# Adding fetched expert rows in the DMA instead of on VectorE, in a one-core macaron layer

## The chip, the core and the metric

The kernel runs on one core of a Trainium2 chip. The core has TensorE (PE, with PEld for its weight loads), VectorE (DVE), ScalarE (ACT), GpSimd (POOL) and SyncE (SP), each with an instruction queue of its own that is worked off in order, and 16 DMA engines that all queues share. SP issues nearly all plain transfers here; POOL issues the indirect ones, whose row addresses come from a tile of indices. The metric is the device time of one execution in microseconds.

## The reference

The input is x with 2 sequences of 4096 tokens and 256 features, in float32. Three blocks are added to it in turn: half of a mixture of experts, a linear attention, and half of the same mixture of experts again.

```python
x = x + 0.5 * _L0_ffn_ref(_layernorm(x), gate_w, w1, w2, w3)
x = x + _L0_attn_ref(_layernorm(x), Wq, Wk, Wv, Wb, ...)
x = x + 0.5 * _L0_ffn_ref(_layernorm(x), gate_w, w1, w2, w3)

def _L0_ffn_ref(x, gate_w, w1, w2, w3):      # 8 experts, two per token
    scores = softmax(xf @ gate_w)
    top_scores, top_idx = top_k(scores, 2)
    scale = zeros((T, E)).at[arange(T)[:, None], top_idx].set(top_scores)
    xs = scale.T[:, :, None] * xf[None, :, :]
    h = silu(einsum('etd,edh->eth', xs, w1)) * einsum('etd,edh->eth', xs, w3)
    y = einsum('eth,ehd->etd', h, w2)
    return y.sum(axis=0)
```

The attention is a gated delta rule with a short convolution and a SiLU in front. It is worked in chunks and carries a state `S` from one chunk to the next.

## The kernel before

The tokens are cut into 16 units. A unit is 256 tokens of each sequence, held as four tiles of 128 tokens with 256 features. For the mixtures of experts, units are put together in groups: 1, 3, 4, 4 and 4 units before the attention (names beginning with `a`), and 4, 4, 4, 3 and 1 after it (names beginning with `b`). A group of one unit is dense: all eight experts run over all its tokens (`all_experts`, L978). Every other group goes through memory in three steps.

- `prepare` (L1041) normalises and routes the tokens. For each of the four tiles of a unit and each of the two choices it makes a tile `row` (the tokens times their score, three buffers under the tag `row`), and an indirect DMA from POOL scatters these rows into `slots` in HBM, so that the rows of one expert lie together (`scatter`, L930).
- `experts` (L1122) loads `slots` two tiles at a time on SP (`xi`), multiplies them with w1 and w3, then with w2, and SP stores the results in `made` in HBM (L1181).
- `combine` (L1183) loads the tokens' own rows `xt` again (L1188). For each tile and each choice, POOL fetches the results of 128 tokens from `made` into a tile `got` with an indirect DMA (`gather`, L948), and DVE adds half of it to the tokens' rows (L1193). `got` shares the tag `row` and its three buffers with the scatter's rows. When all eight fetches of a unit are added, SP stores the block (`leave`, L1032), to `mid1` for the attention or to the output.

There are 30 such units, so 240 scatters, 240 fetches and 240 adds, and every one of them moves 128 rows of 1 KB.

The weights w1, w3 and w2 of all experts lie in one tile `wx_sb`, with w2 in the last 256 columns of each expert. `load_experts` (L676) fills it at the start with five DMAs on SP, and the first dense group is the first to use it. In the dense groups the products with w2 of all experts are summed in PSUM, and one DVE instruction per two tiles adds half of them to the tokens' rows (L1028).

The attention runs beside all this. In it POOL computes powers (`rr` L1498, `nk` L1283, and `rs` L751 for the normalisations) and copies the convolution's carried columns (L1236, L1238). `rr` is the factor that `on` (L1512) applies on DVE before PE transposes `on` into `pto`.

The order of the work is not the order of the source. The instructions are recorded in a `Plan` (L169), step by step, and `Plan.order` (L432) lays them out with costs for each engine (a POOL fetch holds POOL for 1278 ns and lands after 2000 ns plus its size), taking first what has the lowest number among what is ready. The table `TURNS` (L47) adds an offset to that number for each of 1055 steps. An instruction recorded with `either` goes to DVE or ACT, whichever the plan finds free. L202 of the profile is the line of the plan that calls the engines' instructions, and L217, L218, L222 and L223 are the copies placed by `either`; the names of the tiles tell them apart.

Of the kernel before, what the change touches and what calls it, by code (L numbers as in the profile page):

```python
# [36 lines left out]
F32 = mybir.dt.float32  # L37
# [3 lines left out]
ALU = mybir.AluOpType  # L41
# [6 lines left out]
    0: -503, 1: -513, 2: -516, 3: -370, 4: -583, 5: 726, 6: -2518, 7: -130, 8: -302, 9: 87,  # L48
    10: -124, 11: -210, 12: -120, 13: -49, 14: -31, 16: 37, 17: 151, 18: 3947, 19: 159, 20: 180,
    21: 1716, 22: 88, 23: -235, 24: -40, 25: 1464, 26: 884, 27: 1522, 28: 483, 29: 1766, 30: 2462,  # L50
    31: 2582, 32: 3382, 33: 170, 34: -217, 35: 428, 36: -1592, 37: 115, 38: 51, 39: 255, 40: 643,
    41: -669, 42: -210, 43: -509, 44: 505, 45: -127, 46: 91, 47: 1585, 48: 38, 49: 1295, 50: 193,
    51: 1197, 52: 216, 53: -416, 54: 1088, 55: -982, 56: -953, 57: -958, 58: -1515, 59: -1356,
    60: -824, 61: -627, 62: -312, 63: -308, 64: -221, 65: -302, 66: -280, 67: -44, 69: -15,
    70: -62, 71: -145, 72: -50, 73: -46, 74: -1795, 75: -55, 76: -9, 77: 1, 78: 364, 79: 100,
    80: -128, 81: 123, 82: 108, 83: 111, 84: -136, 85: -35, 86: 81, 87: 3, 88: 209, 89: 883,
    90: -104, 91: -82, 92: -14, 93: -22, 94: 222, 95: 298, 96: 1362, 97: 420, 98: -2033, 99: 760,
    100: -48, 101: 25, 102: -85, 103: -2631, 104: -2008, 105: -27, 106: -111, 107: -2148,
    108: 1154, 109: -39, 110: -3637, 111: -2138, 112: -1132, 113: -2221, 114: 21, 115: -1517,
    116: -206, 117: -1803, 118: -1354, 119: -431, 120: -706, 121: 262, 122: -274, 123: -46,  # L60
    124: -191, 125: -192, 126: 422, 127: 1624, 128: 282, 129: 476, 130: -367, 131: 348,
    132: -1154, 133: -780, 134: 44, 135: -614, 136: -460, 137: -333, 138: 67, 139: -480,
    140: -469, 141: -1054, 142: -358, 143: -626, 144: 622, 145: -369, 146: -360, 147: -255,
    148: 396, 149: -432, 150: -147, 151: -170, 152: -32, 153: -7, 154: -43, 156: -10, 157: 68,
    158: -8, 159: 1247, 160: -95, 161: 458, 162: 358, 163: 499, 164: 32, 165: 340, 166: 422,
    167: 647, 168: 198, 169: 492, 170: 549, 171: 500, 173: 576, 174: 1453, 175: 1527, 176: 645,
    177: 427, 178: 1549, 179: 614, 180: -309, 181: 498, 182: -114, 183: -338, 184: 382, 185: -513,
    186: 469, 187: 762, 188: 814, 189: 8, 190: 1130, 191: -495, 192: 370, 193: 2169, 194: -90,
    195: 628, 196: 1176, 197: -53, 198: 2671, 199: 441, 200: 1964, 201: 324, 202: -291, 203: 1998,
    204: 558, 205: -1778, 206: -99, 207: -236, 208: 13, 209: -299, 210: -496, 211: 134, 212: 253,  # L70
    213: -866, 214: 605, 215: -5, 216: -868, 217: 655, 218: -51, 220: 41, 221: 76, 222: -446,
    223: 1126, 224: -1864, 225: -1411, 226: -946, 227: -931, 228: 176, 229: -398, 230: -363,
    231: -1958, 232: -1114, 233: 264, 234: -56, 235: -530, 236: 557, 237: -519, 238: -347,
    239: -51, 240: 158, 241: -137, 242: -215, 243: -234, 244: -269, 245: -136, 246: -433, 247: 23,
    248: -1053, 249: -135, 250: -2056, 251: 123, 252: -1260, 253: -786, 254: -11, 255: -1518,
    256: -135, 257: -1044, 259: -43, 260: 4, 261: 111, 262: 355, 263: -1258, 264: -125, 265: 419,
    266: 246, 267: 83, 268: 66, 269: 30, 270: 282, 271: 48, 272: 342, 273: -585, 274: -1611,
    275: -107, 276: -166, 277: -162, 279: -729, 280: -592, 281: -1401, 282: -604, 283: -383,
    284: -1104, 285: -937, 286: -503, 288: 113, 289: 1177, 290: 546, 291: -209, 292: 350,
    294: 883, 295: 933, 296: 1314, 297: -759, 298: 441, 299: 444, 300: 868, 301: 950, 302: 114,  # L80
    303: 1217, 304: 436, 305: 88, 306: -126, 307: 541, 308: 1618, 309: 165, 310: 2866, 311: 1087,
    312: 359, 313: -25, 314: 931, 315: 29, 316: 922, 317: 115, 318: 1467, 319: 334, 320: 269,
    321: 268, 322: 465, 323: -734, 324: 2, 325: -18, 326: 224, 327: 346, 328: 12, 329: 207,
    330: 396, 331: 306, 332: 432, 333: 157, 334: 385, 335: 124, 336: 384, 337: -18, 338: 1433,
    339: -68, 340: 128, 341: 81, 342: -1578, 343: -120, 344: -552, 345: -466, 346: 1633,
    347: -789, 348: -158, 349: -29, 350: 1347, 351: 264, 352: -603, 353: -1800, 354: 537,
    355: -2390, 356: -2508, 357: -1362, 359: 490, 360: -743, 361: -161, 362: -290, 363: 42,
    364: 1041, 365: -192, 366: 680, 367: -10, 368: -318, 369: -43, 370: 62, 371: 1217, 372: -1254,
    373: -679, 374: -216, 376: -318, 377: -582, 378: 259, 379: -266, 380: -829, 381: -198,
    382: 204, 383: 1523, 384: -80, 385: -1594, 386: 102, 387: -328, 388: -1562, 389: -510,  # L90
    390: 295, 391: -179, 392: -69, 393: 64, 394: -199, 395: -86, 396: -659, 397: -860, 398: -15,
    399: -2434, 400: -685, 401: -25, 402: 145, 403: 49, 404: 284, 405: 540, 406: -1189,
    407: -2502, 408: -477, 409: -171, 410: -99, 411: 80, 412: -220, 413: 272, 414: -816,
    415: -2133, 416: 718, 417: 412, 418: -70, 419: -50, 420: 285, 421: -514, 422: -476, 423: -481,
    424: -17, 425: 1643, 426: 816, 427: -142, 428: 53, 429: -472, 430: -832, 431: 254, 432: -30,
    433: 1608, 434: -459, 435: -605, 436: -98, 437: -309, 438: 368, 439: -500, 440: 105, 441: -73,
    442: -52, 443: 989, 444: 616, 445: 1460, 446: -1346, 447: -1190, 448: -1070, 450: -115,
    451: -291, 452: -772, 453: -91, 454: -1312, 455: -89, 456: -661, 457: 77, 458: 96, 459: 1097,
    460: 788, 461: 234, 462: -284, 463: -255, 464: -109, 465: -503, 466: -526, 467: 881, 468: -35,
    469: 664, 470: 1931, 471: 525, 472: 2711, 473: -124, 475: 169, 476: 2357, 477: 81, 478: 177,  # L100
    479: -167, 480: -547, 481: -142, 482: -101, 483: 1712, 486: -434, 487: 306, 488: 184,
    489: 290, 490: -11, 491: 52, 492: 286, 493: 446, 494: 91, 495: 550, 496: 215, 497: 646,
    498: 1181, 499: 46, 500: -905, 501: -654, 502: 430, 503: -697, 504: -880, 505: -1416,
    506: -120, 507: 500, 508: 298, 509: -2134, 510: 442, 512: -80, 513: -1521, 514: -986,
    515: -723, 516: 79, 517: 243, 518: -198, 519: 76, 520: 124, 521: 84, 522: -178, 523: 367,
    524: 2502, 526: 165, 527: -60, 528: 221, 529: 927, 530: 276, 531: -70, 532: -296, 533: -13,
    534: -67, 535: -712, 536: 128, 537: -170, 538: 120, 539: -9, 540: -30, 541: -107, 542: -148,
    543: -498, 544: 358, 545: -499, 546: -79, 547: 501, 548: 319, 549: -92, 551: 309, 552: -899,
    553: 592, 554: -2484, 555: 11, 556: -499, 557: -256, 558: -129, 559: -452, 560: -116,
    561: -937, 562: 595, 563: 366, 564: -687, 565: 67, 566: 99, 567: -240, 568: 1155, 569: 102,  # L110
    570: -493, 571: -160, 572: 309, 573: 454, 574: -3028, 575: -15, 576: 71, 577: -168, 578: 435,
    580: 550, 581: -178, 582: 1094, 583: -346, 584: -774, 585: 256, 586: 247, 587: -50, 588: -217,
    589: 643, 590: -59, 591: 261, 592: -721, 594: -65, 595: 289, 596: -503, 597: 23, 598: 177,
    599: -106, 600: -96, 601: -347, 602: 123, 603: -91, 604: 533, 605: 204, 606: 230, 607: -692,
    608: -340, 609: -81, 610: -714, 611: 401, 612: 379, 613: 178, 614: -297, 615: 58, 616: 130,
    617: -442, 618: -543, 619: 69, 620: -414, 621: -29, 622: -85, 623: -652, 624: -210, 625: -151,
    626: 189, 627: 31, 628: -71, 629: 102, 630: 122, 631: -395, 632: -4, 633: 162, 634: 204,
    635: 117, 636: -3, 637: 654, 640: -1477, 641: -135, 642: -237, 643: -96, 644: -264, 645: 164,
    646: -221, 647: -180, 649: -591, 650: -24, 651: 771, 652: 121, 653: -16, 654: -717, 655: -79,
    656: 5, 657: 676, 658: 151, 659: -575, 660: -2162, 661: 64, 663: 41, 664: 1075, 665: 464,  # L120
# [431 lines left out]
def kernel(  # L552
# [18 lines left out]
    nc = tc.nc  # L571
    P = 128
    B, L, DM = x.shape
# [1119 lines left out]
```

## Time and profile before

| | |
|---|---|
| time, three runs | median 1911.07 us (1904.27 to 1919.39) |
| the profiled execution | 1918.22 us, its span 1916.4 us |
| mean granted clock of TensorE | 0.934 |
| moved by DMA | 259.48 MB, mean 135 GB/s |
| the queue of POOL's DMAs | 62.95 MB of it |
| POOL, 240 fetches | 241.9 us busy |
| DVE, 240 adds of fetched rows | 101 us busy |

The spans and waits in the text below come from the profiled execution. A row of the trace on POOL is the time in which POOL was busy with a DMA, not the time in which the data moved; when the data has landed is seen from what waits for it. "PE idle" is the length of a stretch minus PE's busy time in it. A wait is put down to the last releaser.

### The profile page before, as it was taken

The page shows a single profiled execution, that of the slowest core. Times are in us where ns is not written, and L with a number is a line of the kernel's source. Part 1 is how long each engine was busy: PE and PEld are TensorE (multiplying, and loading weights), DVE is VectorE, ACT ScalarE, POOL GpSimd, SP SyncE. Part 2 cuts the span into 40 slices and gives each one's busy share as a digit, 9 for nine tenths or more (in the row PEclk, how much of TensorE's full clock was granted, in tenths as well). Part 3 has the DMA queues.
Part 4 walks back from the last instruction along what each step waited for, and adds up shares of the span by engine and source line. Part 5 has one row for each costly group of instructions (what it writes and reads, how often), then busy time and mean ns, then how long its engine had stood idle before and what let it go on. Part 6 is the DMA issues. An engine that isn't in the chain of part 4 may idle for free.

```text
span 1916.4 us, 34449 instructions
## 1 busy us (share of the span) xinstructions
PE 1674.2 (87%) x11656; PEld 1269.5 (66%) x11656; DVE 1238.8 (65%) x4166; ACT 754.5 (39%) x1566; POOL 706.1 (37%) x800
## 2 busy tenths in 40 slices
PE   4878789689989989898999899689899988899898
PEld 2656465566767667676677677567577767777776
DVE  3637568776774795679657667776865777265254
ACT  1435335343343535344443335243352533234332
POOL 2413644453112324623323452331215333353434
PEclk9999989898898989998889989899898999899999
DMA  6173474554132244634223552332246435474673
GB/s 231 50 274 114 167 218 132 176 162 126 49 87 85 79 137 142 188 104 132 78 59 111 158 154 78 114 115 58 67 126 178 130 114 161 156 218 142 203 226 116
DMA packets 296396, 259.48 MB, mean 135 GB/s; under 512 B 117536, under 2 KB 275232, under 8 KB 296224
## 3 DMA queue, kind: packets, MB, share of 16 engines
q1 hardware_dynamic: 271552, 190.13, 32.4%
q0 software_dynamic: 23040, 62.95, 10.1%
q10 hardware_dynamic: 1632, 4.21, 0.6%
q8 instruction: 96, 1.57, 0.3%
q14 instruction: 76, 0.62, 0.1%
HBM read 137.52 MB, written 119.67 MB: 134 GB/s over the span
## 4 chain that ended last, share of the span: by engine, by line
PE 51%; DVE 19%; DMA 11%; issue 9%; ACT 5%; POOL 3%; SPq 1%; another core or an unknown queue 1%; POOLq 0%; ACTq 0%; DVEq 0%
PE po L202 5%; PE pj_a L202 4%; PE pb_a L202 3%; PE p_a L1109 3%; DMA got_b<-made,sli_b 3%; DVE cv_a L202 3%; PE p_b L1109 3%; DMA got_a<-made,sli_a 3%; PE pmid L202 3%; PE py_b L1109 3%; PE py_a L1109 2%; PE pyo L202 2%; PE pg L202 2%; PE pz L202 2%; PE p_b L202 1%
## 5 line engine op out<-in xcount | busy, mean ns | idle before, releaser
L202 DVE SCALAR_TENSOR_TENSOR cv_a<-pre_a,cw_sb,cv_a 128x512 f32<-128x512 f32 x288 | 212.6, 745 | 7.5 <-ACT cv_a L223 3.5
L202 PE MATMUL pj_a<-xT_a,wp_sb 128*128 128x512 f32 x384 | 196.0, 614 | 7.7 <-DVE xT_a L217 2.9
L934 POOL DMA_INDIRECT slots<-row_b,sli_b x120 | 121.2, 1010 | 203.2 <-DVE sli_b L202 78.7
L1109 PE MATMUL p_a<-wx_sb,xiT_a 128*128 x608 | 159.2, 399 | 17.7 <-ACT xiT_a L218 5.2
L934 POOL DMA_INDIRECT slots<-row_a,sli_a x120 | 121.1, 1009 | 126.5 <-issue 49.5
L1109 PE MATMUL p_b<-wx_sb,xiT_b 128*128 x608 | 158.1, 394 | 8.2 <-ACT xiT_b L218 3.8
L952 POOL DMA_INDIRECT got_b<-made,sli_b x120 | 117.7, 981 | 125.8 <-issue 21.8
L952 POOL DMA_INDIRECT got_a<-made,sli_a x120 | 124.2, 1035 | 85.3 <-issue 21.5
L1109 PEld LDWEIGHTS p_a<-wx_sb,xiT_a 128*128 128x128 f32 x608 | 115.4, 199 | 48.4 <-issue 10.9
L1109 PEld LDWEIGHTS p_b<-wx_sb,xiT_b 128*128 128x128 f32 x608 | 110.9, 194 | 31.8 <-ACT xiT_b L218 7.2
L202 POOL TENSOR_TENSOR rr<-ms,mhalf 128x8 f32<-128x8 f32 x32 | 54.2, 1693 | 120.3 <-DVE ms L202 120.1
L1109 PE MATMUL py_a<-wx_sb,hT_a 128*128 x304 | 87.2, 407 | 9.6 <-DVE hT_a L217 2.8
L202 PE MATMUL po<-mid,at 128*128 128x64 f32 x512 | 92.7, 316 | 2.7 <-ACT mid L218 1.4
L202 PEld LDWEIGHTS po<-mid,at 128*128 128x128 f32 x512 | 89.3, 244 | 7.7 <-ACT mid L218 3.8
L202 PE MATMUL pmid<-r,XT 128*128 128x64 f32 x512 | 74.1, 306 | 21.1 <-DVE r L202 9.4
L202 PEld LDWEIGHTS pj_a<-xT_a,wp_sb 128*128 128x128 f32 x384 | 65.0, 193 | 41.1 <-issue 24.4
L202 POOL TENSOR_TENSOR rs_a<-ve_a,mhalf 128x4 f32<-128x4 f32 x32 | 34.2, 1070 | 154.0 <-DVE ve_a L202 153.8
L1109 PE MATMUL py_b<-wx_sb,hT_b 128*128 x304 | 88.0, 412 | 2.2 <-DVE ms L202 0.9
L202 PEld LDWEIGHTS pmid<-r,XT 128*128 128x128 f32 x512 | 70.7, 219 | 28.4 <-DVE r L202 13.0
L202 POOL COPY pre_a<-carry 128x6 f32<-128x6 f32 x96 | 28.7, 299 | 161.5 <-DVE cv_a L202 137.8
L202 DVE TENSOR_TENSOR yb<-yb,z 128x31 f32<-128x31 f32 (+15 forms) x248 | 84.2, 339 | 5.1 <-DVE run_a L202 0.6
L202 DVE TENSOR_TENSOR z<-lb,yb 128x31 f32<-128x31 f32 (+15 forms) x248 | 83.7, 337 | 4.2
(290 smaller groups left out, 3894.2 us busy)
## 6 DMA issues: line engine op xcount, KB each, us to landing
xi_a<-slots SPq DMA_DIRECT2D x76, 256.0 KB
made<-yo_a SPq DMA_DIRECT2D x76, 256.0 KB
xi_b<-slots SPq DMA_DIRECT2D x76, 256.0 KB
made<-yo_b SPq DMA_DIRECT2D x76, 256.0 KB
x_a<-in_L_attn_x_dram SPq DMA_DIRECT2D x32, 256.0 KB
x_a<-mid SPq DMA_DIRECT2D x16, 512.0 KB
xr<-mid SPq DMA_DIRECT2D x64, 128.0 KB
mid<-xr SPq DMA_DIRECT2D x64, 128.0 KB
```

What stands on the lines that cost most here:

```text
L202: self.plan.add(self.name, lambda: real(*args, **kw), ins, outs, cost)
L934: ins = tc.nc.gpsimd.indirect_dma_start(out=dst, out_offset=bass.IndirectOffsetOnAxis(ap=slot, axis=0), in_=row, in_offset=None,)
L952: return tc.nc.gpsimd.indirect_dma_start(out=got, out_offset=None, in_=src, in_offset=bass.IndirectOffsetOnAxis(ap=slot, axis=0),)
L1109: return tc.nc.tensor.matmul(o, lhsT=lhsT, rhs=wx_sb.rearrange("p e c -> p (e c)")[:, cols], start=start, stop=stop,)
```

## The change

The fetch becomes an accumulating DMA: it reads the results from `made` and adds them to the tokens' rows in SBUF. Its destination is the tile of `xt` itself, so `got` and the 240 DVE adds are gone, and the tag `row` is left to the scatters. The factor one half moves into w2: after the load, one instruction multiplies w2 by 0.5 in place, on DVE or ACT, and the dense groups add their sum without a factor. In `combine` the loops over choices and tiles change places, so that the four tiles' first choices are fetched first and then the four second ones. The plan records the fetch with `xt` as a thing read and written. The table TURNS is replaced as a whole by another of the same kind.

```diff
 TURNS = {
-    0: -503, 1: -513, 2: -516, 3: -370, 4: -583, 5: 726, 6: -2518, 7: -130, 8: -302, 9: 87,
...
+    1054: 865,
 }
...
         nc.sync.dma_start(wx_sb[:, :, 2 * KC * FH :], w2.rearrange("e f d -> f e d"))
 
+        down = wx_sb[:, :, 2 * KC * FH :]
+        nc.either.copy(down, down, 0.5)
+
...
-    def gather(g, got, slot):
+    def gather(g, xt, slot):
+
         src = made[g.par][0 : g.ntl * P, :]
 
         def call():
             return tc.nc.gpsimd.indirect_dma_start(
-                out=got,
+                out=xt,
                 out_offset=None,
                 in_=src,
                 in_offset=bass.IndirectOffsetOnAxis(ap=slot, axis=0),
-            )
-
-        plan.add("gpsimd", call, [src, slot], [got], plan.dma(got, 4 * DM, True))
+                compute_op=ALU.add,
+            )
+
+        plan.add("gpsimd", call, [src, slot, xt], [xt], plan.dma(xt, 4 * DM, True))
...
             xa = xt[:, a : a + 2, :]
-            nc.vector.scalar_tensor_tensor(xa, py, 0.5, xa, ALU.mult, ALU.add)
+            nc.vector.tensor_tensor(xa, py, xa, ALU.add)
             yield 1.0
...
             xt = load(g.src, u, f"{g.name}_{i}c")
-            for a in range(NT):
-                for k in range(2):
-                    got = wk.tile([P, DM], F32, tag="row", name=f"got_{g.name}_{i}_{a}_{k}", bufs=3)
-                    gather(g, got, g.slot[i][:, a, k : k + 1])
-                    nc.vector.scalar_tensor_tensor(
-                        xt[:, a, :], got, 0.5, xt[:, a, :], ALU.mult, ALU.add
-                    )
+            for k in range(2):
+                for a in range(NT):
+                    gather(g, xt[:, a, :], g.slot[i][:, a, k : k + 1])
             leave(g, u, xt)
             yield 0.5
```

## The prediction

> **What bounds the kernel now.** I read the busy table first, then the chain of waits, then the stretches in which results are fetched, and last the fetches and what stands around them. Busy time and chain:
>
> ```profile
> PE 1674.2 (87%) x11656; PEld 1269.5 (66%) x11656; DVE 1238.8 (65%) x4166; ACT 754.5 (39%) x1566; POOL 706.1 (37%) x800
> PE 51%; DVE 19%; DMA 11%; issue 9%; ACT 5%; POOL 3%; SPq 1%; another core or an unknown queue 1%; POOLq 0%; ACTq 0%; DVEq 0%
> ```
>
> PE is busy for 87% of the span, so nothing off PE is worth more than the 242 us in which PE stands still, some of them in the start, where weights arrive. The chain's second line names fetched rows twice, at 3% each, some 110 us. They are not worth that: the chain follows the last releaser even where PE is full beside it. So I went to the eight stretches that hold the 240 fetches (found from the POOL rows by time). Columns: length, busy time of PE, PEld, DVE, ACT, POOL with counts, granted clock, DMA share, GB/s.
>
> ```profile
> 227.00:276.00 49.00, 36.76 (x159) 28.59 (x160) 25.74 (x79) 14.16 (x29) 30.64 (x31) 0.85 0.69 212
> 373.00:443.00 70.00, 60.73 (x494) 43.56 (x495) 50.70 (x118) 25.01 (x48) 42.24 (x48) 0.92 0.59 171
> 753.00:816.00 63.00, 55.52 (x384) 39.29 (x383) 38.31 (x91) 23.18 (x47) 42.40 (x44) 0.97 0.62 185
> 1069.00:1145.00 76.00, 70.80 (x639) 55.13 (x637) 44.77 (x114) 24.62 (x51) 43.37 (x46) 0.87 0.56 158
> 1438.00:1520.00 82.00, 75.26 (x534) 56.54 (x532) 53.51 (x133) 28.91 (x58) 41.61 (x48) 0.90 0.55 161
> 1654.00:1716.00 62.00, 56.15 (x417) 46.44 (x415) 35.59 (x116) 21.24 (x46) 35.34 (x35) 0.94 0.69 214
> 1795.00:1856.00 61.00, 54.65 (x275) 43.61 (x274) 27.19 (x90) 24.64 (x52) 32.03 (x33) 0.97 0.80 244
> 1871.00:1909.00 38.00, 34.28 (x160) 26.39 (x161) 18.29 (x52) 10.28 (x31) 23.90 (x24) 1.00 0.41 125
> sum 501.00, PE 444.13 PEld 339.55 DVE 294.09 ACT 172.04 POOL 291.53; mean PE 55.52 PEld 42.44 DVE 36.76 ACT 21.50 POOL 36.44
> ```
>
> In these 501 us PE is idle for 57, or 11%. In the 1333 us between 60 and 1795 us outside them it is busy for 1182, again 11% idle. Fetching starves PE no more than the rest does. Then single rows: the POOL instruction (min/median/max in ns), the queue that carries scatters and fetches, two steps of the chain (start, length), two waits (total, times, longest), the last combine's first and last fetch, and the last add.
>
> ```profile
> L952 POOL DMA_INDIRECT got_b<-made,sli_b x120: 943/958/1282, 1438.6 to 1905.3; - x120
> q0 software_dynamic: 23040, 62.95, 10.1%
> 1810.02 2.46 DMA got_b<-made,sli_b
> 1847.35 6.13 DMA got_b<-made,sli_b
> DVE x_b_0c L202 <- DMA got_b<-made,sli_b: 27.2, 16, 5.6
> PE pto L202 <- DVE on L202: 16.2, 10, 6.8
> 1871.29 0.96 POOL L952 DMA_INDIRECT got_b<-made,sli_b  x1 [16.10 <-DVE hs_b L202]
> 1905.32 0.96 POOL L952 DMA_INDIRECT got_b<-made,sli_b  x1 [0.30 <-issue]
> 1912.33 0.69 DVE x_b15c L202
> ```
>
> A fetch lands 2.5 to 6.1 us after its issue (eight such steps between 1795 and 1853 us, mean 4.6). Back to back, POOL issues one each 0.96 + 0.30 = 1.26 us. The end is close: last fetch at 1905, PE's last product to 1912, span 1916.
>
> **The change part by part.**
>
> Removed, DVE work: 240 adds at 0.42 us (rows of 0.417 to 0.425) are 101 us, a third of DVE's 294 us in the stretches. Removed with them: DVE's in-order waits for fetched rows, 97 us over the eight groups of adds (27.2 above is the largest). They freed no PE: in 1795 to 1856 us DVE waits 27 us for rows, while PE idles 6.4, and of that only 3.1 by DVE (for hs). So I let 40% of the 57 us go, not all: the rest is ACT copies, loads and dependences inside the blocks, which stay. 0.4 x 57 = 23 us. In the first stretch the clock is 0.85 with PE at 75%, against a mean of 0.934; half of the way back on 37 us of PE work is 2 us. Gain 25.
>
> Removed, POOL waits: with three row buffers shared by scatters and fetches, a fetch waits for an add three fetches earlier. The waits of fetches on adds sum to 74 us and on earlier fetches to 15. They go. What is late next is the second choice's fetch: it adds into a row block that the first choice's fetch must have finished. The loop now runs four first choices, then four second ones, so 4 x 1.26 = 5.0 us lie between the two. At a landing of 4.6 nothing waits, at 6.1 it waits 1.1. Behind it on POOL stand the powers for rs, rr and nk and the carry copies, and behind rr waits PE by way of `on` (16.2 us now).
>
> Here the skill speaks against the change. "DMA: Bandwidth & Descriptors", Rules for kernel authors, says that an accumulating DMA reads its destination and writes it later with nothing held in between, so an earlier accumulate's semaphore must be waited for. By the landing row that costs 0 to 1.1 us per unit, 30 units; I take 0.5, so 15 us of POOL, which has 210 us of slack in the stretches: 2 us on the path.
>
> Added, the accumulation itself: no row shows one. Nearest row: the plain fetch, 0.96 us of POOL, and for the transfer 10.1% x 1916 / 480 = 0.40 us of all 16 engines. "Collectives: The Full Stack", in the section on the bandwidth ceiling, says that a DMA's addition costs no cycles but a second source read, with two read descriptors per piece, and that this halves the rate. By the row the change adds nothing. By the rule a transfer takes 0.8 us, 97 us more over 240 in a DMA system at 45% mean share, and the landing is 0.4 later. If POOL writes those descriptors, three in place of two, its 0.96 becomes 1.45 (an estimate from that page and the row). I take the rule for the transfer, the row for POOL. Both ends on POOL stay for the range: 0.96, and double. The engine's addition below the row's cost is excluded, as it moves at least the same bytes.
>
> Stores: SP's store of a finished block used to wait for the last add (76 us in all) and now waits for the last landing. The add and its signal, some 0.5 us, go, 0.4 comes: nothing. Behind it on SP stand the loads of expert rows; PE waits 10.3 us for those today. If landing grew to 9 us, 30 x (9 - 4.6) = 132 us of SP would block; at the 11% by which PE is uncovered, 15 us.
>
> Moved: the first fetch now needs the tokens' rows, which only the first add needed. Their loads go out at 179 us for the fetch at 228, and 1833.8 for 1871.3: hidden by more than 30 us.
>
> Added, the halving of w2: 128 x 2048 in one instruction. By the 128 x 512 scaling of `wo_sb` at 0.48 us, 1.9 on DVE; by four ACT copies of 0.585, 2.3. The first product with w2 is at 49.8 us, and DVE idles 18.7 us before 31.6. Hidden; standing behind w2's arrival on the wrong engine it costs up to 2.3. I take 1. The dense adds keep their shape and time: nothing.
>
> The order: TURNS is another table, so every engine's queue is another order of the same work. No row prices that. Bound: a fifth of the 151 us of PE idle outside the stretches either way, 30 us; value 0.
>
> Sum: -25 + 2 + 1 = -22 on the profiled execution's 1918.22 us, or 1896. That execution lies 7 us above the median of 1911.07, so the median should come to **1889 us**.
>
> **The rivals.**
>
> The fetch becomes dear on POOL (slower). Place: the last combine. From 1871.3 to 1916.4 there are 45 us; the last landing (4.6) and store (3.4, from the last add's end at 1913.0) take 8 of them, so 24 fetches have 37 us, 1.55 us each. Above that step POOL sets the end. At 2.2 us a step (0.96 doubled, with the 0.30) the tail runs 24 x 2.2 - 37 = 16 over. The three densest stretches of 32 fetches (61 to 63 us) overrun by some 8 each, 25; later rr, rs and nk powers cost PE about as much again as it waits behind `on` today, 16. With the gain spent: 1911 + 57 = 1968. For it: three descriptors, unknown software. Against it: POOL is at 58% in the stretches, and the plain fetch leaves 0.29 us to spare.
>
> PE keeps its time: the DVE and POOL waits were under PE's cover, and an awkward order or late landing (15 us above) takes the rest. 1911 - 22 + 17 = 1906. For it: 11% idle inside and outside alike.
>
> The change doesn't do what it says: accumulations into quarters of one block are kept apart as if they hit the same bytes, eight landings in a row, 8 x 5 = 40 us a unit; the tail alone grows from 37 to 120. About 2000 or more. Little speaks for it: the two halves of such a block are already loaded by separate DMAs.
>
> **How the numbers follow.** Likeliest, fetch near today's price: 0.45, own range 1858 (60% of the idle time gone, 11 us more, and 20 us of the order's 30) to 1905, of which 0.05 falls within 1%. PE keeps its time: 0.18, within 1%. Dear fetch: 0.33, 1930 to 2000. Serial fetches: 0.04. A measurement here can tell about 1%, 19 us, from no change. Faster 0.40, same 0.23, slower 0.37. The range runs from that **1858** to **1972**, which takes in the dear fetch at 1968; outside are a very good order (0.07) and the worse dear and serial cases (0.13).
>
> **What would show it.** Right: no `got` tiles, DVE busy near 1138 us, POOL rows of the fetch at 0.96 to 1.45 us, landings under 6.5, PE idle in the stretches near 34 us, waits on earlier fetches under 20 us in all. Wrong: POOL rows of the fetch near 2 us, the last fetch later than 1912 us with PE done, second fetches waiting 3 us and more each, or DVE and POOL relieved as said and PE's idle time unchanged.

## The result and the profile after

The changed kernel takes 2087.86 us (median of 4 runs, 2080.43 to 2089.88), beside 1907.67 us for the kernel before on the same chip (4 runs): a ratio of 1.097, 95% interval 1.089 to 1.105. That is 180 us slower, where 22 us faster was forecast. The profiled execution of after took 2086.84 us, with a span of 2084.9 us.

Busy time, the queue that carries scatters and fetches, and the chain by engine, from the page of after:

```profile
PE 1694.6 (81%) x11656; PEld 1284.4 (62%) x11656; DVE 1151.4 (55%) x3925; ACT 751.6 (36%) x1568; POOL 832.4 (40%) x800
q0 software_dynamic: 46080, 62.95, 14.5%
PE 43%; DVE 18%; issue 13%; POOL 12%; DMA 8%; ACT 4%; SPq 1%; another core or an unknown queue 0%; POOLq 0%; DVEq 0%; ACTq 0%
```

DVE lost 87 us of work; the adds that went had been 101 us, so some of its other rows grew. POOL gained 126 us with the same 800 instructions, the queue moved the same 62.95 MB in twice as many packets, and POOL's share of the chain went from 3% to 12%. PE does the same 11656 products and stands still for 390 us, against 242.

The row of one of the fetch groups, in min/median/max ns, and three waits behind POOL's small powers (total, times, longest, in us):

```profile
L959 POOL DMA_INDIRECT x_b_1c<-made,sli_b x32: 1531/1541/1549, 1540.5 to 2063.8; - x32
```

```profile
DVE x_b L205 <- POOL rs_b L205: 59.3, 5, 29.0
DVE on L205 <- POOL rr L205: 49.8, 18, 32.2
PE pto L205 <- DVE on L205: 44.2, 11, 30.9
```

The accumulating fetch holds POOL for 1.54 us where the plain one held it for 0.96. And work that waits for POOL's small powers (`rs`, `rr`) now waits up to 32 us at a time. Before, the wait for `rs_b` was 1.5 us in all, and the one for `rr` was:

```profile
DVE on L202 <- POOL rr L202: 32.9, 20, 4.0
```

The number of waits is about the same. What grew is the longest one, from 4.0 to 32.2 us.

The stretches that hold the fetches, five of the eight and the sum of all, in the same columns as before the change:

```profile
228.00:276.00 48.00, 28.91 (x121) 22.30 (x120) 9.71 (x38) 10.04 (x22) 40.80 (x27) 0.79 0.81 181
...
1135.00:1202.00 67.00, 39.10 (x311) 29.47 (x310) 21.21 (x41) 12.38 (x26) 54.24 (x42) 0.66 0.67 124
1533.00:1596.00 63.00, 33.52 (x292) 25.95 (x290) 12.97 (x30) 12.23 (x25) 53.91 (x36) 0.79 0.73 140
...
1926.00:1987.00 61.00, 26.36 (x122) 21.18 (x122) 7.44 (x22) 9.69 (x22) 50.68 (x33) 0.77 0.76 155
2034.00:2085.00 51.00, 40.14 (x186) 31.23 (x184) 11.66 (x32) 12.03 (x35) 37.07 (x24) 0.97 0.57 103
sum 485.00, PE 293.81 PEld 224.99 DVE 124.47 ACT 105.56 POOL 395.24; mean PE 36.73 PEld 28.12 DVE 15.56 ACT 13.19 POOL 49.41
```

The stretches are no longer than before (485 us against 501), but PE works for 294 us of them instead of 444. 191 us of PE's idle time now lie here, 134 more than before, and the clock granted in the six middle ones is 0.66 to 0.80 where it was 0.87 to 0.97. The work that PE did not do here it does later, and the span grows. The last stretch, where the prediction had put the place of the dear fetch, grew by only 6 us (45 to 51).

One stretch shows how. First before, then after: POOL's rows around the one power `rs_b` that is computed while a layer's 32 fetches run (start, length, instruction, idle time before it and what ended it), in after with the two instructions that waited for it.

```profile
1819.75 0.95 POOL L952 DMA_INDIRECT got_b<-made,sli_b  x1 [1.15 <-DVE x_b_1c L202]
1821.01 0.95 POOL L952 DMA_INDIRECT got_b<-made,sli_b  x1 [0.31 <-DVE st_b L202]
1822.97 1.08 POOL L202 TENSOR_TENSOR rs_b<-ve_b,mhalf 128x4 f32<-128x4 f32 x1 [1.02 <-DVE ve_b L202]
1824.25 1.14 POOL L952 DMA_INDIRECT got_b<-made,sli_b  x1 [0.20 <-DVE x_b_1c L202]
```

```profile
1982.07 1.55 POOL L959 DMA_INDIRECT x_b_3c<-made,sli_b  x1 [0.30 <-issue]
1983.92 1.55 POOL L959 DMA_INDIRECT x_b_3c<-made,sli_b  x1 [0.30 <-issue]
1984.91 1.63 POOL L205 TENSOR_TENSOR rs_b<-ve_b,mhalf 128x4 f32<-128x4 f32 x1
1986.58 1.38 DVE L205 TENSOR_SCALAR x_b<-x_b,mv_b,rs_b 128x256 f32<-128x256 f32 x4 [28.32 <-POOL rs_b L205]
1987.10 2.03 PE L205 MATMUL ptx_b<-ident,x_b 128*128 128x128 f32 x8 [24.58 <-issue]
```

Before, fetches wait in between for an add to free a row buffer, and `rs_b` goes out after 16 of the 32, as soon as its input is there. After, no wait for a row buffer stands between the fetches; all 32 go out one every 1.85 us, `rs_b` comes after the last, DVE waits 28 us for it and PE stands for 24.6. The trace says "issue" for PE. The product that it starts at 1987.10 reads the `x_b` that DVE wrote just before, and DVE's row names what was late.

So there were two suspects, and a third behind them: the price of 1.54 us, the order in which POOL issues, and the new table `TURNS`. On POOL the order written by the plan does not bind: the kernel asks for a manual schedule of PE, DVE, ACT and SP alone (L1645), so POOL's instructions take the places that the framework gives them.

### The profile page after: what moved, and what is told of

Its sections match the earlier page's. It is cut to its first block, busy times and chain, and to the rows that moved or that the text cites. A ratio compares the mean times of both kernels' runs of the same rounds, so it can differ in the third digit from the quotient of the medians.

```text
span 2084.9 us, 34013 instructions
## 1 busy us (share of the span) xinstructions
PE 1694.6 (81%) x11656; PEld 1284.4 (62%) x11656; DVE 1151.4 (55%) x3925; ACT 751.6 (36%) x1568; POOL 832.4 (40%) x800
## 3 DMA queue, kind: packets, MB, share of 16 engines
q0 software_dynamic: 46080, 62.95, 14.5%
## 4 chain that ended last, share of the span: by engine, by line
PE 43%; DVE 18%; issue 13%; POOL 12%; DMA 8%; ACT 4%; SPq 1%; another core or an unknown queue 0%; POOLq 0%; DVEq 0%; ACTq 0%
PE po L205 4%; DVE cv_a L205 4%; PE p_b L1117 4%; PE pj_a L205 3%; PE p_a L1117 3%; PE py_b L1117 2%; PE pmid L205 2%; PE pyo L205 2%; PE py_a L1117 2%; PE pb_a L205 2%; DVE z L205 2%; POOL x_a_2c L959 1%; DVE yb L205 1%; POOL x_a_1c L959 1%; PE pds L205 1%
## 5 line engine op out<-in xcount | busy, mean ns | idle before, releaser
L205 DVE SCALAR_TENSOR_TENSOR cv_a<-pre_a,cw_sb,cv_a 128x512 f32<-128x512 f32 x288 | 211.8, 745 | 18.5 <-POOL pre_a L205 14.5
L205 PE MATMUL pj_a<-xT_a,wp_sb 128*128 128x512 f32 x384 | 201.4, 628 | 7.8 <-DVE cv_a L225 3.1
L1117 PE MATMUL p_a<-wx_sb,xiT_a 128*128 x608 | 164.4, 410 | 13.2 <-ACT xiT_a L221 7.9
L205 POOL COPY carry<-pre_a 128x6 f32<-128x6 f32 x96 | 28.8, 307 | 233.8 <-ACT pre_a L221 233.3
L221 ACT COPY pre_a<-pj_a 128x512 f32<-128x512 f32 x90 | 52.7, 586 | 85.0 <-PE pj_a L205 65.2
```

Of the source, the lines that this page charges most:

```text
L205: self.plan.add(self.name, lambda: real(*args, **kw), ins, outs, cost)
L221: lambda: nc.scalar.copy(out, in_),
L1117: return tc.nc.tensor.matmul(o, lhsT=lhsT, rhs=wx_sb.rearrange("p e c -> p (e c)")[:, cols], start=start, stop=stop,)
```

## The experiments

The experiments ran in groups at different times, each with the kernel before beside them. Before's median was between 1842 and 1920 us in these groups, so kernels of different groups are compared by their ratio to before in their own group, and a difference of two ratios is turned into time with 1907.67 us. That a ratio of one group holds in another is assumed: no kernel but before ran in two of them.

### First round: the price or the order

**e1_plain.** The fetch without the accumulate:

```diff
                 in_offset=bass.IndirectOffsetOnAxis(ap=slot, axis=0),
-                compute_op=ALU.add,
             )
```

> The kernel after, its fetches without the accumulate: each of the 240 fetches overwrites the tokens' rows in place of adding to them (the accumulation is left out), everything else and the order of issue as in after. Theory price (the accumulating fetch holds POOL 1.54 us against 0.96, and 240 of them make the loss): POOL's row of the fetch falls back to about 0.96 us and the time to 1890 to 1920. Theory unbroken run (without row buffers nothing paces the fetches, so the 32 of a layer go out before POOL's powers and copies, whatever one costs): the run of 32 shortens only from 59 to 41 us, the time stays at 2000 or more. Theory layout (the new table of turns is a worse order, whatever the fetch costs): 2000 or more too, with the loss outside the fetch stretches.

Measured: 2065.98 us, 1.082 (1.074 to 1.090). POOL's fetch row fell back to 0.96 us and the stretches to 368 us, yet the time fell by 22 us only. Nearly the whole loss stays with the cheap fetch, as the theories of the unbroken run and of the layout both had it. This spoke against the price, but the run had waits of its own, shown below under plain_pin, so it prices nothing cleanly.

**a_pin.** The kernel after with POOL held in the plan's order. Each POOL instruction gets an edge, without a semaphore, to those that the plan has ahead of it:

```diff
-            call[e]() if isinstance(call, dict) else call()
+            ins = call[e]() if isinstance(call, dict) else call()
+            if e == "gpsimd":
+                self.pin(ins, self.ops[k][5] is not None)
+
+    def pin(self, ins, scatter):
+        ins = getattr(ins, "ins", ins)
+        for other in self.fixed if scatter else self.fixed + self.loose:
+            self.tc.add_manual_dep(
+                ins,
+                other.name,
+                mybir.DependencyInfo(mybir.DependencyClass.NoSync, mybir.DependencyReason.DATA),
+                reason="the plan's order on GpSimd",
+            )
```

> The kernel after, with POOL's instructions held in the plan's order (edges without a semaphore between POOL's instructions), the fetch as dear as before. Theory unbroken run: POOL's powers and copies now stand between the fetches where the plan has them, a large part of the loss comes back, 1930 to 1990. Theory price: the fetches hold POOL for the same 375 us, and the stretches stay starved, 2040 to 2100.

Measured: 1973.70 us, 1.035 (1.026 to 1.044). With the fetch as dear as in after (POOL busy 836.5 us), nearly two thirds of the loss is gone. The longest waits for `rs_b` and `rr` are 9.0 and 12.5 us, against 29.0 and 32.2.

**told_pin.** The same, and the plan is told a higher cost:

```diff
-                free[e] = t + (1278 if soft else 430)
+                free[e] = t + ((price if price > 1 else 1278) if soft else 430)
...
-        plan.add("gpsimd", call, [src, slot, xt], [xt], plan.dma(xt, 4 * DM, True))
+        plan.add("gpsimd", call, [src, slot, xt], [xt], plan.dma(xt, 4 * DM, 1850))
```

> As the kernel after with POOL held in the plan's order, and the plan is told 1850 ns for a fetch on POOL in place of 1278, so that the order of all engines is laid out for what the trace shows. Theory layout: clearly below the run that only holds POOL's order, 1900 to 1960. Theory price: an order can't give back what POOL's 440 us in the stretches take; within 30 us of that run, above 2000.

Measured: 1992.63 us, 1.046 (1.039 to 1.054), no better than a_pin; the 1900 to 1960 of the layout theory did not come. Telling the true price to the plan brings nothing while the table of turns stays the one that was made for 1278 ns. That alone does not clear the table.

**b_pin.** The control: the same hold on the kernel before.

> The kernel before, with POOL's instructions held in the plan's order in the same way: what holding the order does by itself. All theories: its three row buffers already pace the fetches, so 1890 to 1925, no change; if holding POOL's order costs something by itself it is seen here, above 1930.

Measured: 1893.82 us, 0.994 (0.991 to 0.997). Before loses nothing by being held, it gains 0.6%. POOL left free costs before 11 us and costs after 119 (after against a_pin). That its row buffers are what kept POOL near the plan's order fits the waits shown above, but no run tests it by itself: before with more row buffers and POOL free was not run.

### Second round: price and table apart

**a_bord.** The work of after in the order of before on all engines, written out as a list, POOL held:

```diff
-        order, span = self.order([k + TURNS.get(s, 0) for k, s in enumerate(self.steps)])
+        raw = zlib.decompress(base64.b85decode(ORDER))
+        n, k, order = len(raw) // 3, 0, []
+        for i in range(n):
+            k += int.from_bytes(raw[2 * i : 2 * i + 2], "little", signed=True)
+            order.append((k, ("sync", "scalar", "vector", "gpsimd", "tensor")[raw[2 * n + i]]))
```

> The work of the kernel after (accumulating fetches, no adds, w2 halved) issued in exactly the order of the kernel before on every engine, POOL held to it too, the 240 adds left out of it. Theory layout (before's order was fitted to the program with its pacing buffers, the new table gives up the rest): the remaining loss against before goes, 1880 to 1920. Theory price (POOL's 1.54 us a fetch is what is left of the loss): 1940 to 1990, as with the new table and POOL held.

Measured: 2194.82 us, 1.143 (1.131 to 1.156), worse than anything before it; neither theory had this. POOL's rows show why:

```profile
1859.11 1.55 POOL L1124 DMA_INDIRECT x_b_1c<-made,sli_b  x1 [0.30 <-issue]
1863.16 1.55 POOL L1124 DMA_INDIRECT x_b_1c<-made,sli_b  x1 [2.50 <-DMA x_b_1c<-made,sli_b]
1865.01 1.55 POOL L1124 DMA_INDIRECT x_b_2c<-made,sli_b  x1 [0.30 <-PE phs_b L348]
1869.13 1.55 POOL L1124 DMA_INDIRECT x_b_2c<-made,sli_b  x1 [2.57 <-DMA x_b_2c<-made,sli_b]
```

Before's order has both choices of a row block one behind the other. Into a row buffer each that is free; as accumulates into the same rows, the second fetch of a pair holds POOL until the first has landed: 116 such waits, 333 us in all, half of them under 2.6 us and the longest 6.6. The swapped loops of the change (second choices after four first ones) are a needed part of it.

**plain_bord.** The same without `compute_op`.

> The same order as before's, but the fetches do not accumulate (they overwrite the tokens' rows; the accumulation is left out), so POOL pays 0.96 us and there is one read of 1 KB a row. It prices what the change should have saved by leaving out adds and buffers: price theory 1870 to 1900, and the distance to the accumulating kernel in the same order is the price of the accumulate, some 60 us; layout theory: within 20 us of the accumulating one.

Measured: 2014.54 us, 1.048 (1.038 to 1.059). It has the same serial pairs, so it is no measure of the saving either; the step to a_bord mixes the price with longer landings.

**plain_pin.** a_pin without `compute_op`.

> The kernel after in its own new order with POOL held to it, fetches not accumulating (left out: they overwrite). Fourth corner of order by price. Price theory: 1890 to 1915, the loss of 66 us that stays with POOL held goes away with the price. Layout theory: stays at 1950 or above, as the order is the same.

Measured: 2033.92 us, 1.056 (1.044 to 1.068): with a cheaper fetch, slower than a_pin. The chain of this run and two of its waits:

```profile
PE 54%; DVE 17%; DMA 7%; issue 7%; another core or an unknown queue 7%; ACT 5%; POOL 2%; SPq 1%; DVEq 0%; ACTq 0%; POOLq 0%
ACT hs_b L205 <- remote: 33.7, 3, 22.9
DVE xiT_a L220 <- remote: 27.9, 1, 27.9
```

7% of the chain, some 140 us, is time in which ACT or DVE waited for something that no record names, up to 28 us at once, while a run of plain fetches went out at 1.26 us each. The same is seen in e1_plain (5%), hardly in after (0%) or a_pin (1%). The seven waits of over 18 us in the two runs all end 2.5 to 4.8 us after the last fetch of an unbroken run has left POOL, about the time in which a fetch lands. In e1_plain, PE too sends its 32x32 products out singly meanwhile, with gaps of up to 3.3 us that the trace puts to nothing. So the waits go with the runs of plain fetches; what is late in them stays open. It makes these two runs useless as a price of the accumulate.

**b_fill.** The kernel before, POOL held, with a small power behind each fetch. Its tile `fill` (128x2) is set to 1.0 once at the start and used by nothing else:

```diff
-            return tc.nc.gpsimd.indirect_dma_start(
+            fetch = tc.nc.gpsimd.indirect_dma_start(
...
+            plan.pin(fetch, False)
+            return tc.nc.gpsimd.tensor_tensor(
+                fill, fill, mhalf.to_broadcast([P, 2]), ALU.pow
+            )
```

> The kernel before, POOL held in its order, with a power on a 128x2 tile right behind each of the 240 fetches, which holds POOL some 0.6 to 0.7 us more per fetch as the accumulate does; transfers, buffers and adds as before. If POOL's time by itself is the price: 1930 to 1980, against 1894 with POOL held and no fill. If the second read and the longer transfer are the price: within 15 us of 1894.

Measured: 1980.88 us, 1.031 (1.020 to 1.043), 71 us over b_pin by the ratios (each interval is about 1% to either side here, or 20 us). The power was dearer than meant, as its row (busy us, mean ns) says:

```profile
L979 POOL TENSOR_TENSOR fill<-fill,mhalf 128x2 f32<-128x2 f32 x240 | 186.8, 778 | 7.4
```

187 us of POOL, with transfers and adds untouched, cost 71 us of the time: POOL's time by itself counts, at 0.38 us per us, though POOL is busy for less than half of the span.

### Third round: before's order, rightly paired

**a_bord2.** a_bord, but inside each unit's eight places the first choices stand ahead of the second ones.

The edit lies in the list `ORDER`, which was made so:

```diff
+    places = sorted(place[k] for k in unit)
+    for q, k in zip(places, unit):
+        order[q] = (k, "gpsimd")
```

> As the kernel in before's order that came out at 2195, but inside each unit's eight places in that order the four first choices stand before the four second choices, so that no fetch waits on POOL for the landing of the fetch just ahead of it. If serial landings were what made 2195: 1960 to 2000, some 200 us lower (120 pairs at about 1.7 us each and what stood behind them). If before's order itself doesn't fit the dearer fetch: still above 2050.

Measured: 1874.11 us where before took 1848.44, 1.013 (1.009 to 1.017). By the ratio that is 1933 us beside 1907.67, below the 1960 to 2000 expected. The serial pairs had cost 0.130, 248 us. And with before's order and POOL held, the change as such loses 1.3%, not 9.7%.

**b_thin.** b_pin with its order fixed and each add cut to 2 columns:

```diff
-                        xt[:, a, :], got, 0.5, xt[:, a, :], ALU.mult, ALU.add
+                        xt[:, a, 0:2], got[:, 0:2], 0.5, xt[:, a, 0:2], ALU.mult, ALU.add
```

> The kernel before with POOL held and its order of issue fixed, each of the 240 adds cut to two columns of 256 (the rest of the addition is left out), fetches, row buffers and waits as before. What the removed adds are worth by themselves. My prediction's step (some 23 us of PE idle in the fetch stretches, 2 us of clock): 1865 to 1880 against 1894 with POOL held. If DVE's adds lie wholly beside other work: 1890 to 1900.

Measured: 1821.75 us where before took 1848.44, 0.986 (0.980 to 0.993): 0.8% below b_pin, 15 us, the low end of what my prediction's step expected (14 to 29 us). The two intervals overlap (0.980 to 0.993 and 0.991 to 0.997), so this says that the adds were partly on the path, and their size only roughly.

### Fourth round: closing the sum

**a_bord2_free.** a_bord2 without the hold on POOL, everything else the same.

> The work of the kernel after in before's order with first choices ahead of second choices, as in the kernel that came out at 1.013 of before, but POOL's instructions not held: they take the places that the framework gives them, as in the kernel after. Theory POOL order (the fetches run ahead of powers and copies only because nothing holds them): the ratio rises to 1.04 or more. Theory table (the new table of turns made the loss): it stays within 1.00 to 1.03.

Measured: 1998.81 us where before took 1843.06, 1.085 (1.079 to 1.091). Same work, same order on four engines, same price of the fetch; POOL's order alone makes 0.072 of a ratio, 137 us; with the new table the same step, a_pin to after, is 0.063, 119 us. The waits of the two kernels, held first:

```profile
DVE on L348 <- POOL rr L348: 39.7, 22, 6.6
PE pto L348 <- DVE on L348: 30.5, 14, 7.0
DVE x_b L348 <- POOL rs_b L348: 11.0, 8, 2.7
```

```profile
PE pto L348 <- DVE on L348: 99.1, 12, 28.0
DVE on L348 <- POOL rr L348: 98.0, 23, 29.8
DVE x_b L348 <- POOL rs_b L348: 48.5, 5, 28.9
```

The number of waits is alike; the longest is four to eleven times as long when the powers stand behind the run of fetches.

**a_found and b_found.** A search for another order with the plan's own costs, the same time for each: for after's work with POOL held and a fetch of 1850 ns, and for before with POOL held. The edit is another list `ORDER`.

> The work of the kernel after with POOL held and an order of issue searched anew for a fetch of 1850 ns on POOL, from before's order. If the loss that is left over before's order (1.013 against 0.994 with POOL held) is a matter of order: below 0.995. If it is POOL's time for the accumulate: 1.00 to 1.02.

> The kernel before with POOL held and an order searched anew with the same effort: the control for the searched order of the accumulating kernel, and the candidate to beat both. A better order is worth something by itself: 0.98 to 0.99; none: 0.99 to 1.00, as with POOL held alone.

Measured: a_found 1.027 (1.017 to 1.037), b_found 0.997 (0.994 to 1.001). The searched order does not bring the changed kernel under before, nor under the order taken over from before (1.013), and b_found does not beat b_pin. That was one search each, by costs that did not foretell the measured order of the kernels; a better order for the changed kernel is not excluded. The left-over loss is therefore put to the accumulate by the next run and not by these.

**plain_bord2.** a_bord2 without `compute_op`, the one clean price of the accumulate.

> The kernel at 1.013 of before (before's order, first choices first, POOL held) with fetches that do not accumulate (left out: they overwrite the tokens' rows). It prices the accumulate by itself with everything else equal. If POOL's 0.6 us more a fetch is what is left of the loss: 0.975 to 0.99 of before. If the price doesn't matter once POOL's order is right: 1.00 to 1.015. A run of plain fetches may again leave ACT and DVE waiting for something the records don't name, as in the other kernels without the accumulate; if it does, the chain shows it as an unknown queue and the time is not a price.

Measured: 1791.91 us where before took 1842.13, 0.972 (0.969 to 0.975), a little better than expected. No unnamed waits here (the chain has none). The sums over the seven stretches that hold the fetches here (the last two of the eight run together), first with and then without the accumulate:

```profile
sum 523.00, PE 452.74 PEld 350.63 DVE 229.13 ACT 181.30 POOL 425.24; mean PE 64.68 PEld 50.09 DVE 32.73 ACT 25.90 POOL 60.75
```

```profile
sum 427.00, PE 403.88 PEld 311.75 DVE 211.57 ACT 167.96 POOL 280.27; mean PE 57.70 PEld 44.54 DVE 30.22 ACT 23.99 POOL 40.04
```

PE is idle for 70 us of the stretches with it and for 23 without. The accumulate costs 0.041 of a ratio, 79 us.

## Why the prediction was wrong

The runs give the whole way from before to after, one thing at a time, in ratios to before: 1.000; POOL held 0.994 (-11 us); adds, row buffers and their waits out, w2 halved 0.972 (-43 us); fetches accumulate 1.013 (+79 us); POOL's order let go 1.085 (+137 us); the new table 1.097 (+23 us). The sum is +185 us by the ratio (180 by the medians). Each step joins runs of two groups and carries some 0.5 to 1% of uncertainty, and the last one is within it: the intervals of after and of a_bord2_free overlap. With POOL held, the new table costs 0.022, 41 us (a_pin against a_bord2), and there the intervals are apart.

- *"Removed, POOL waits ... They go. What is late next is the second choice's fetch."* This is the step that failed most. The waits went, and second choices rarely wait (4.3 us in all for the one group that shows it in after). But with them gone and POOL's order left to the framework, the fetches ran ahead of POOL's powers and copies; the waits, it seems, had done a second job. I named the powers, and that PE waits behind `rr`, and then priced 0.5 us for each of 30 units, 2 us on the path. What came is a run of 32 fetches, 59 us, ahead of them. The step ended at the instruction that waits next, and did not ask what else issues sooner once nothing waits. Measured: 137 us.
- *"I take the rule for the transfer, the row for POOL."* The rule of the Trainium skill ("Collectives: The Full Stack", the section on the bandwidth ceiling) that an accumulate reads a second source with a descriptor of its own is told there of a collective's reduce. Twice the packets and about twice the transfer time fit it; the bytes on record (62.95 MB in both) show no second read. Taking the 240 scatters at an unchanged 0.40 us each, the queue's 14.5% of 2084.9 us is 302 us of all engines, so 0.86 us for a fetch, against the 0.8 taken. And POOL's 1.45 us, worked out from that page and set aside for the nearest row, met a measured 1.54. The row was near in shape but not in kind. With 1.45 the sum would have had 240 x 0.49 = 118 us more of POOL, with the measured 1.54 it is 240 x 0.58 = 139; by b_fill's 0.38, measured only afterwards, these are 45 and 53 us, and the measured price is 79. What the other 26 us are (longer landings are one candidate) no run separated.
- *"POOL, which has 210 us of slack in the stretches."* Slack by busy time is no slack for an engine whose short instructions others wait for. b_fill spends 187 us of it and loses 71.
- *DVE near 1138 us:* 1151 measured. It shows that the adds are gone, not that anything waited for them.
- *The 40% of 57 us that PE would get back*, and 2 us of clock: right in kind; the 25 us of gain lie between two measured values. Adds alone are worth some 15 us (b_thin); adds, buffers and their waits together 43 (plain_bord2 against b_pin), and PE's idle time in the stretches falls from 56 us in b_pin to 23. The other 28 us would be the freed buffers' and their waits'. The prediction put those at nothing on the path; but the 28 are a difference of two runs that also holds the halved w2 and the new places of the second choices, not a run of its own.
- *"The order: TURNS ... value 0", bound 30 us:* 23 us measured with POOL free and 41 with it held, around the bound. The bound spoke of queues of the same work in another order; POOL's order, which no table sets, was not in it.
- *The rival "dear fetch".* Its mechanism came true, its place did not. At a step of 1.85 us its formula gives 24 x 1.85 - 37 = 7 us for the tail, and 6 were measured. It gave 25 us to the dense stretches and 16 to the powers, where nearly all of the loss arose. *"PE keeps its time"* is refuted by plain_bord2, where PE is idle for 23 us in the stretches instead of 56. *"Serial fetches"* is not what the change does, but a_bord shows it with its price, 248 us.
- *Moved, the first fetch needs the tokens' rows*, *stores* and *w2*: no wait of size showed for the first and the last. SP's waits to store a finished block rose from 76 us (for adds) to 126 (for landings) in after. In a_bord2 whatever of that is left lies within its 1.3%.

The version that beats both, by little, is the kernel before with POOL held in the plan's order: 0.994 (0.991 to 0.997), 11 us.

## What to carry to other kernels

A wait for a buffer may also be what keeps a queue in order: before taking it away, ask what its engine will issue sooner, and which short instruction then stands behind a long run. An order written out by hand covers only the engines that it is declared for; look in the program at the others. And an operation that differs in kind from the nearest row (an accumulate from a copy) is taken at the rule's price until a row of its own is there.

## What the runs showed of the hardware

- An indirect fetch of 128 rows of 1 KB that adds into SBUF holds POOL for 1.54 us, a plain one for 0.96; the step between two is 1.85 against 1.26 us, as 0.30 us lie between in both.
- The same bytes go in 46080 packets instead of 23040. If scatters and fetches had 48 packets each before, and the scatters keep theirs, a fetch goes from 48 to 144, three times as many.
- Two accumulates into the same rows, one behind the other, leave POOL standing between them: 2.57 us in the median of a_bord's 116 waits, 6.6 at most.
- Where a layer's plain fetches go out in unbroken runs, ACT and DVE can stand for up to 29 us for something that no record names (e1_plain, plain_pin); with another order (plain_bord2) it did not happen. The longest of these waits end soon after the run's last fetch, 2.5 to 4.8 us; the cause is open.
